# A graph layer on one core: the head of the kernel in an order set by hand, with a table of its own for the first quad of nodes

## The chip, the cores and the metric

The kernel runs on one core of a Trainium2 chip. The metric is device microseconds from the first to the last instruction of that core, as a median over runs; lower is better. The engines are named as in the profile: PE (matrix products, with PEld its weight loads), DVE (vector), ACT (scalar), POOL (GpSimd) and SP, which here only issues transfers. Each engine takes its instructions in the order in which the program gives them to it.

## The reference, cut to what matters

There are 12,500 nodes with 128 features and 412,500 edges. Edges are sorted by `dst`; `src` is in no order.

```
h    = relu(layernorm(x)) @ W_in2f
Wij  = (ssp(edge_attr @ W_f1 + b_f1) @ W_f2 + b_f2) * edge_weight[:, None]   # ssp(t) = softplus(t) - log 2
agg  = segment_sum(h[dst] * Wij, src, 12500)
out  = x + ssp(agg @ W_o1 + b_o1) @ W_o2 + b_o2
```

So each edge reads a row of `h` at its `dst`, multiplies it by a filter made from its 20 attributes, and adds the product to node `src`.

## The kernel before, in words

Nodes are worked on in 25 quads of 512 (the last one is shorter). `make_h(q)` is a generator that makes the rows of `h` for one quad in seven pieces: layer norm statistics on DVE (L310, L311) and the inverse root on ACT (L314, L315); the normalising on DVE (L326); transposes on PE (L331) and `relu` on ACT (L333); the product with `win` on PE (L337); then a split of the result into three bfloat16 parts, on ACT and DVE by turns (L339 to L345); then the stores on SP (L352, L359). The stores go to `h3`, and to tables `h3_q`, one for each quad: table q holds the rows of quad q with a margin of 256 rows before it and 384 after it. A quad therefore writes to up to three tables, and table 0 is complete only when quads 0 and 1 are both stored.

Edges are worked on in 806 chunks of 512, four chunks to a group. Since `dst` is sorted, the rows of `h` that a chunk needs lie in a window of 32 rows. `shift` holds where that window starts for each of the 808 chunks; `rel_d` holds, for each edge, its row within the window. Both come from `dst_c`: `relative()` computes `shift` from the first `dst` of each chunk (`first`, a load of 808 single elements, L155), and `rel` from seven loads of 128 chunks each (L160), which it writes to `rel_d` (L277). `ranges` checks later that all edges were in their windows.

`step(k)` issues the work of several chunks at different stages, in one fixed order. For chunk k + 12 the group's loads of attributes, `rel`, `src` and `edge_weight` (in `Group.__init__`, L542 to L556); for k + 6 the window load `near` (`rows`, L569 and L571), which reads a register from `shift`; for k + 7 and k + 6 the search for a free slot for each edge (`columns`, `blocks`, `rank`, `rank_end`: L578 to L606, L636, L655 and L687 on PE, L660); for k + 4 to k + 2 the first layer of the filter (`hidden`, `hidden_log`, `hidden_end`: L616, L619, L620, L625, L631); for k + 2 the selection matrix `at` (`window`, L706); for k + 1 the second layer of the filter `v` (L726, L730) and the picked rows `hg` (L714, L719); and for k the message: `o = v * hg` on DVE (L741), and four indirect stores on POOL (L745), each of which scatters 128 messages to their slots in `slots`. `o` has 4 buffers, each for two chunks, so that DVE waits at L739 for the scatters of eight chunks before. Later units of work (`Collect`) load the slots back and add them up with PE (L807), segment by segment, and `finish` makes the output. Its loads of `x` for the first three quads (`xo`, L387, and the addition of `bo2`, L401) need nothing from the loop, and stand at the head of the program.

The order of the head was left to the scheduler: constants, weights and their loads (on SP), the loads of `dst_c` (on ACT's queue), the bias parts (L246 to L253). Within `with tc.manual_schedule()` the order is the program's own:

```
h = [make_h(q, psum) for q in range(2)]
for m in h + h:
    next(m)
aside = side()
relative()
while h:                     # both quads to their end, by turns
    ...
for k in range(-LG, ...):    # LG = 12
    ...
    step(k, now)
    next(aside, None)
```

`side()` starts a further `make_h` every nine steps, from quad 2 on, beginning in step −12. Transfers issued from SP and ACT take eight semaphores in turn, so each transfer waits for the one eight before it in the program's order.

Of the kernel before, what the change touches and what calls it, by code (L numbers as in the profile page):

```python
# [31 lines left out]
EPS = 1e-5  # L32
NEAR = 2 * P
# [7 lines left out]
def gnn_kernel(  # L41
# [33 lines left out]
    NFLAG = 6 * len(SEGS) + 8  # L75
# [39 lines left out]
    ident = const.tile([P, P], F32, name="ident")  # L115
    make_identity(nc, ident)
    eps = const.tile([P, 1], F32, name="eps")
    nc.vector.memset(eps, EPS)
    half = const.tile([P, 1], F32, name="half")
    nc.vector.memset(half, 0.5)  # L120

    nc.scalar.preload_act_table_set("natural_log_exp_and_others")


    ln = ctx.enter_context(tc.tile_pool(name="ln", bufs=2))
    QN = QT * P
    NQ = ceil_div(N, QN)

# [12 lines left out]
    early = {q: load_x(q) for q in range(2)}  # L141

    state = ctx.enter_context(tc.tile_pool(name="state", bufs=1))
    early_room = state.tile([P, NTILE * P], F32, name="early_room", tag="agg")
    NC = NG * NCHUNK
    NPART = ceil_div(NG * NCHUNK, P)
    rel = early_room[:, NPART * CH:NPART * CH * 3 // 2 + CH].bitcast(BF16)
    rel = rel[:, :NPART * CH].rearrange("p (k e) -> p k e", e=CH)
    rows_at = NPART * CH * 3 // 2 + CH

    def early_row(k):
        return early_room[0:1, rows_at + k * NC:rows_at + (k + 1) * NC]

    first = early_row(0).bitcast(I32)
    nc.scalar.dma_start(first, dst_c[:, 0:1].rearrange("c o -> o c"))  # L155
    parts_c = []
    for c0 in range(0, NC, P):
        n = min(P, NC - c0)
        dc = early_room[:, len(parts_c) * CH:(len(parts_c) + 1) * CH].bitcast(I32)
        nc.scalar.dma_start(dc[:n, :], dst_c[c0:c0 + n, :])  # L160
        parts_c.append((c0, n, dc))


    quad_of = [min(c * CH * N // (n_edges * QN), NQ - 1) for c in range(NC)]

    def base_of(q):
        return max(0, q * QN - NEAR)

    def rows_of(q):
        return (q + 1) * QN + NEAR + P - base_of(q)  # L170

    base, last_w, strays, kept_in = (early_row(k) for k in range(1, 5))
    for q in range(NQ):
        cs = slice(quad_of.index(q), quad_of.index(q) + quad_of.count(q))
        nc.gpsimd.memset(base[:, cs], float(base_of(q)))
        nc.gpsimd.memset(last_w[:, cs], float(rows_of(q) - WR))

    def load(ap, shape, name):
        t = const.tile(shape, F32, name=name)
        nc.sync.dma_start(t, ap)  # L180
        return t

    win = load(w_in2f, [P, P], "win")

    before = const.tile([P, P], F32, name="before")
    nc.gpsimd.memset(before, 1.0)
    nc.gpsimd.affine_select(out=before, in_=before, compare_op=ALU.is_ge, fill=0.0, base=-1,
                            pattern=[[-1, P]], channel_multiplier=1)
    spare = const.tile([P, 1], F32, name="spare")
    nc.gpsimd.iota(spare, pattern=[[1, 1]], base=N, channel_multiplier=1,  # L190
                   allow_small_or_imprecise_dtypes=True)
    wf2 = load(w_f2, [P, P], "wf2")
    wo1 = load(w_o1, [P, P], "wo1")
    wo2 = load(w_o2, [P, P], "wo2")
    bf1 = load(b_f1[:, None], [P, 1], "bf1")
    bo1 = load(b_o1[:, None], [P, 1], "bo1")
    bf2 = load(b_f2[None, :].to_broadcast([P, P]), [P, P], "bf2")
    bo2 = load(b_o2[None, :].to_broadcast([P, P]), [P, P], "bo2")

    wf1 = const.tile([P, P], F32, name="wf1")  # L200
    for j in range(NCHUNK):
        nc.sync.dma_start(wf1[32 * j:32 * j + RBF, :], w_f1)

    def spread(t, n):
        return t[:, None, :].to_broadcast([t.shape[0], n, P])


    WP = 3 * WR
    prow_i = early_room[:WP, rows_at + 5 * NC:rows_at + 5 * NC + CH].bitcast(I32)
    nc.gpsimd.iota(prow_i, pattern=[[0, CH]], base=0, channel_multiplier=43)  # L210
    nc.vector.tensor_scalar(prow_i, prow_i, 7, None, op0=ALU.logical_shift_right)
    prow = const.tile([WP, CH], BF16, name="prow")
    nc.vector.tensor_copy(prow, prow_i)
    ones = const.tile([P, 1], F32, name="ones")
    nc.vector.memset(ones, 1.0)

    h3 = tc.dram_tile([NTILE * P, 3 * P], BF16, name="h3")
    h3_q = [tc.dram_tile([rows_of(q), 3 * P], BF16, name=f"h3_{q}") for q in range(NQ)]
    rel_d = tc.dram_tile([NC, CH], BF16, name="rel_d")
    flag = const.tile([1, 1], I32, name="flag")  # L220

    after = const.tile([P, P], F16, name="after")
    nc.gpsimd.memset(after, 1.0)
    nc.gpsimd.affine_select(out=after, in_=after, compare_op=ALU.is_ge, fill=0.0, base=-1,
                            pattern=[[1, P]], channel_multiplier=-1)
    nc.vector.scalar_tensor_tensor(after, ident, BIG, after, op0=ALU.mult, op1=ALU.add)

    rest_of = const.tile([P, P], F16, name="rest_of")
    nc.vector.tensor_scalar(rest_of, after, -1.0, 1.0, op0=ALU.mult, op1=ALU.add)
    ones_b = const.tile([P, P], BF16, name="ones_b")  # L230
    nc.vector.memset(ones_b, 1.0)

    turn = const.tile([P, NCHUNK, QT], F32, name="turn")
    for t in range(QT):
        nc.vector.memset(turn[:, :, t:t + 1], -1.0 if t % 2 else 1.0)
    places = const.tile([P, P], F32, name="places")
    nc.gpsimd.iota(places, pattern=[[1, P]], base=0, channel_multiplier=0,
                   allow_small_or_imprecise_dtypes=True)
    nbf1 = const.tile([P, 1], F32, name="nbf1")
    nc.vector.tensor_scalar(nbf1, bf1, -1.0, None, op0=ALU.mult)  # L240

    bf2_p = const.tile([3, P], BF16, name="bf2_p")
    left = const.tile([1, P], F32, name="bf2_left")
    with tc.tile_pool(name="bias_ps", bufs=1, space=PSUM) as bias_ps:
        b12 = bias_ps.tile([1, P], F32, name="b12")
        nc.tensor.matmul(b12, bf1, wf2, start=True, stop=True)  # L246
        nc.vector.tensor_add(left, b12, bf2[0:1, :])
    for k in range(3):
        part = const.tile([1, P], BF16, name=f"bf2_{k}")
        nc.vector.tensor_copy(part, left)  # L250
        if k < 2:
            nc.vector.tensor_sub(left, left, part)
        nc.sync.dma_start(bf2_p[k:k + 1, :], part)  # L253
    zero = const.tile([P, ZR * RW], F32, name="zero")
    nc.gpsimd.memset(zero, 0.0)
    bad = const.tile([1, NFLAG], F32, name="bad")
    nc.vector.memset(bad, 0.0)
    sums = tc.dram_tile([SUMT * P, P], F32, name="sums")
    segs = [Segment(k) for k in range(len(SEGS))]


    shift = const.tile([1, NC], I32, name="shift")

    def relative():
        nc.vector.tensor_sub(strays, first, base)
        nc.vector.tensor_scalar(kept_in, strays, 0.0, None, op0=ALU.max)
        nc.vector.tensor_tensor(kept_in, kept_in, last_w, op=ALU.min)
        nc.vector.tensor_copy(shift, kept_in)
        nc.vector.tensor_tensor(strays, strays, kept_in, op=ALU.not_equal)
        nc.vector.tensor_reduce(bad[:, NFLAG - 1:], strays,  # L270
                                axis=mybir.AxisListType.X, op=ALU.max)
        nc.vector.memset(rel[:, NPART - 1, :], 0.0)
        for k, (c0, n, dc) in enumerate(parts_c):
            d0 = ln.tile([P, 1], F32, name="d0")
            nc.vector.tensor_copy(d0[:n, :], dc[:n, 0:1])
            nc.vector.tensor_scalar(rel[:n, k, :], dc[:n, :], d0[:n, :], None, op0=ALU.subtract)
            nc.scalar.dma_start(rel_d[c0:c0 + n, :], rel[:n, k, :])  # L277

    def ranges(psum):
# [10 lines left out]
        nc.vector.tensor_reduce(worst, ends, axis=mybir.AxisListType.XY, op=ALU.max)  # L290
        nbad = psum.tile([P, QT, P], F32, name="nbad", tag="acc")[:1, 0, :1]
        nc.tensor.matmul(nbad, worst, ones, start=True, stop=True)
        nc.vector.tensor_copy(bad[:, NFLAG - 2:NFLAG - 1], nbad)


    none = const.tile([P, 3 * P], BF16, name="none")
    nc.vector.memset(none, 0.0)

    def make_h(q, psum):

        n = min(QT, NTILE - q * QT)
        xb = early.pop(q, None)
        if xb is None:
# [182 lines left out]
    with tc.tile_pool(name="edge", bufs=2) as edge, tc.tile_pool(  # L486
# [447 lines left out]
        def side():  # L934

            h = []
            for i in range(1000):
# [5 lines left out]
                if i == 40:  # L943
                    h.append(ranges(psum))
# [92 lines left out]
```

## Time and profile before

| what | value |
|---|---|
| median of 3 runs | 4383.54 us (4381.74 to 4402.45) |
| profiled execution, its own time | 4396.31 us |
| its span in the trace | 4394.5 us |
| mean granted clock of PE | 0.855 |
| busy: PE, DVE, ACT, POOL | 82%, 71%, 53%, 71% |
| transfers | 829.10 MB, mean 189 GB/s |
| first scatter starts, last scatter starts | 85.08 us, 4220.62 us |

In the rows of the timeline the columns are start and duration in microseconds, engine, line, operation and tiles; in brackets stands how long the engine had been idle and what ended that. In the rows of the windows they are the stretch, its length, the busy time of each engine with its number of instructions, the granted clock of PE, the busy share of the DMA engines and GB/s. An engine name with a q is the queue that issues for it.

### The profile page before, as it was taken

The page shows a single profiled execution, that of the slowest core. Times are in us where ns is not written, and L with a number is a line of the kernel's source. Part 1 is how long each engine was busy: PE and PEld are TensorE (multiplying, and loading weights), DVE is VectorE, ACT ScalarE, POOL GpSimd, SP SyncE. Part 2 cuts the span into 40 slices and gives each one's busy share as a digit, 9 for nine tenths or more (in the row PEclk, how much of TensorE's full clock was granted, in tenths as well). Part 3 has the DMA queues.
Part 4 walks back from the last instruction along what each step waited for, and adds up shares of the span by engine and source line. Part 5 has one row for each costly group of instructions (what it writes and reads, how often), then busy time and mean ns, then how long its engine had stood idle before and what let it go on. Part 6 is the DMA issues. An engine that isn't in the chain of part 4 may idle for free.

```text
span 4394.5 us, 72656 instructions
## 1 busy us (share of the span) xinstructions
PE 3607.4 (82%) x22558; PEld 2618.3 (60%) x22558; DVE 3140.1 (71%) x6637; ACT 2332.5 (53%) x4685; POOL 3114.6 (71%) x3288
## 2 busy tenths in 40 slices
PE   3767776777777888888788889999899998989877
PEld 2544444444444666666566567777677776767666
DVE  5766666566555776767667678787888878888766
ACT  3655555555555555555555555555555555545424
POOL 2777777677777777777777777777777777777620
PEclk9776666667666898899998899999999999999999
DMA  5766547888765666765876566666666766766666
GB/s 139 192 178 230 174 128 197 223 223 230 183 208 135 177 178 183 238 193 166 257 197 174 150 179 187 194 195 185 189 188 183 199 191 185 193 188 191 172 180 192
DMA packets 498071, 829.10 MB, mean 189 GB/s; under 512 B 170680, under 2 KB 288300, under 8 KB 497676
## 3 DMA queue, kind: packets, MB, share of 16 engines
q1 hardware_dynamic: 378950, 602.34, 51.2%
q0 software_dynamic: 103168, 213.15, 14.7%
q10 hardware_dynamic: 15558, 8.89, 0.7%
q8 instruction: 182, 2.98, 0.3%
q14 instruction: 213, 1.74, 0.1%
HBM read 425.03 MB, written 398.98 MB: 188 GB/s over the span
## 4 chain that ended last, share of the span: by engine, by line


## 5 line engine op out<-in xcount | busy, mean ns | idle before, releaser
L745 POOL DMA_INDIRECT slots<-o,slot x3224 | 3108.4, 964 | 1106.3 <-issue 803.6
L719 ACT ACTIVATE hg<-picked,rcut 128x128 f32<-128x128 f32 x3224 | 920.8, 369 | 1372.0 <-PE picked L714 1323.5
L807 PEld LDWEIGHTS acc<-to,m 128*128 128x128 f32 x8312 | 1078.7, 205 | 353.8 <-issue 187.7
L807 PE MATMUL acc<-to,m 128*128 128x128 f32 x8312 | 1154.6, 294 | 92.3 <-DVE agg L824 47.3
L730 PEld LDWEIGHTS v<-wf,r 128*128 128x128 f32 x6448 | 918.1, 220 | 303.7 <-issue 303.7
L730 PE MATMUL v<-wf,r 128*128 128x128 f32 x6448 | 1088.2, 320 | 0.0
L616 PE MATMUL z<-f,wf 20*128 20x512 f32 x1612 | 524.2, 726 | 217.5 <-DVE r L631 190.9
L794 DVE TENSOR_TENSOR to<-count_ps,m 128x768 f32<-128x768 f32 (+3 forms) x829 | 657.9, 812 | 51.8 <-PE acc L807 27.7
L619 ACT ACTIVATE a<-z,bf 128x1024 f32<-128x1024 f32 x403 | 449.1, 1114 | 426.7 <-PE z L616 426.7
L660 DVE TENSOR_REDUCE top<-free 128x4 f32<-128x392 f32 x806 | 447.2, 555 | 211.7 <-PE free L655 210.4
L631 DVE SCALAR_TENSOR_TENSOR r<-z,nbf,a 128x1024 f32<-128x1024 f32 x403 | 514.6, 1277 | 94.2 <-ACT a L625 92.5
L741 DVE TENSOR_TENSOR o<-v,hg 128x512 f32<-128x512 f32 x806 | 547.2, 679 | 2.8 <-ACT hg L719 2.1
L739 DVE COPY o<-place 128x8 f32<-128x8 f32 x403 | 80.4, 200 | 650.9 <-DMA slots<-o,slot 650.6
L714 PE MATMUL picked<-near,at 96*128 96x128 bf16 x3224 | 356.4, 240 | 218.0 <-DVE o L741 215.7
L625 ACT ACTIVATE a<-a,half 128x1024 f32<-128x1024 f32 x403 | 468.4, 1162 | 0.0
L636 DVE TENSOR_TENSOR inb<-count_ps,blk 128x392 f16<-128x392 f32 x806 | 445.7, 553 | 0.0
L726 PE MATMUL v<-bf_p,ones_b 3*128 3x512 bf16 x806 | 350.1, 434 | 104.1 <-DVE o L741 93.9
L620 ACT ACTIVATE a<-a 128x1024 f32<-128x1024 f32 x403 | 425.9, 1057 | 12.8
L714 PEld LDWEIGHTS <-at 96*128 96x128 bf16 x3224 | 275.7, 109 | 256.2 <-DVE o L741 224.6
L616 PEld LDWEIGHTS z<-f,wf 20*128 20x128 f32 x1612 | 142.4, 206 | 388.9 <-issue 186.3
L687 PE MATMUL free<-inb,rest_of 128*128 128x392 f16 x806 | 303.1, 376 | 55.0 <-DVE top L660 53.8
L706 DVE TENSOR_TENSOR at<-rel,prow 96x512 bf16<-96x512 bf16 x806 | 331.1, 411 | 0.0
(107 smaller groups left out, 1416.2 us busy)
## 6 DMA issues: line engine op xcount, KB each, us to landing
m<-slots SPq DMA_DIRECT2D x371, 387.0 KB
rel<-rel_d SPq DMA_DIRECT2D x202, 384.0 KB
m<-slots SPq DMA_DIRECT2D x172, 322.5 KB
m<-slots SPq DMA_DIRECT2D x212, 258.0 KB
slots<-o,slot POOLq DMA_INDIRECT x3224
slots<-zero SPq DMA_DIRECT2D x24, 2064.0 KB
f<-in_f_t SPq DMA_DIRECT2D x404, 80.0 KB
slots<-zero SPq DMA_DIRECT2D x22, 1032.0 KB
```

What stands on the lines that cost most here:

```text
L616: nc.tensor.matmul(z[:, k, :], wf1[rows, :], self.f[rows, :], start=True, stop=True)
L619: nc.scalar.activation(a, z, AF.Abs, bias=bf1)
L625: nc.scalar.activation(a, a, AF.Ln, bias=half, scale=0.5)
L631: nc.vector.scalar_tensor_tensor(r, z, nbf1, a, op0=ALU.max, op1=ALU.add)
L660: nc.vector.tensor_reduce(self.top[:, c * QT:(c + 1) * QT], free_v, axis=mybir.AxisListType.X, op=ALU.max)
L714: nc.tensor.matmul(ps[:, i, :], at[:, i * P:(i + 1) * P], near, start=True, stop=True)
L719: nc.scalar.activation(hg[:, i, :], ps[:, i, :], AF.Copy, scale=self.rcut[:, j:j + 1])
L730: nc.tensor.matmul(v[:, i, :], r[:, i * P:(i + 1) * P], wf2, start=False, stop=True, skip_group_check=True)
L741: nc.vector.tensor_mul(o[:, :, :P], v, hg)
L745: put = nc.gpsimd.indirect_dma_start(out=views[j % VIEWS], out_offset=bass.IndirectOffsetOnAxis(ap=self.slot[:, j:j + 1], axis=0), in_=o[: ...
L794: nc.vector.tensor_tensor(to[:, :n, :], count_ps[:, None, :].to_broadcast([P, n, P]), self.m[u][:, :n, P:].to_broadcast([P, n, P]), op=ALU ...
L807: nc.tensor.matmul(self.acc[b // QT][:, i, :], m[:, j, :P], to[:, j, :], start=t == 0, stop=t == self.seg.tiles(b) - 1)
```

## The change

The head is moved into functions that are called within the manual order. `constants()` loads quad 0 of `x`, the first part of `dst_c`, the first elements of 64 chunks (`FIRST`), `win`, `wf1` (all on SP), and `bf1`, `wf2`, `bf2` (on ACT), and sets the constants. Then come quad 0's first pieces, `relative(0)` and `shift(0)`, which serve 128 and 64 chunks. The loop over steps begins at that point: quad 0's other pieces, the loading and making of quad 1, and the bias parts (`biases`) are issued between the steps −12 to 0. `side()` begins in step 0. What is left goes into `rest()`, a generator which `side()` starts at its sixth call: the first elements of the other 744 chunks, `wo1`, `wo2`, `bo1`, `bo2`, `shift(1)` for 744 chunks, then the other six parts of `dst_c` one after another (load, `relative`, store), and at the end `ranges`. The loads and stores of `dst_c` and `rel_d` are now on SP's queue. In `Group.__init__` the load of `rel` comes after those of attributes, `src` and `edge_weight`.

There is a new first table, of the rows of quad 0 alone; chunks 0 to 8 use it. The other 25 tables are as they were. `make_h` stores to the new table first, and has one more piece after that.

The loads of `xo` stay at the head of ACT's queue, and the additions of `bo2` to them, which need `bo2`, now stand on DVE in step 8, between the operations of `shift(1)`.

```diff
+FIRST = 64
+    tables = [(0, QN)]
+    for q in range(NQ):
+        start = max(0, q * QN - NEAR)
+        tables.append((start, (q + 1) * QN + NEAR + P - start))
+    table_of = []
+    for c in range(NC):
+        n = c * CH * N // n_edges
+        table_of.append(0 if n < QN - NEAR - P else min(n // QN, NQ - 1) + 1)
...
-    early = {q: load_x(q) for q in range(2)}
...
+    def constants():
+        early[0] = load_x(0)
+        part_load(0)
+        first_load(0)
+        nc.sync.dma_start(win, w_in2f)
+        for j in range(NCHUNK):
+            nc.sync.dma_start(wf1[32 * j:32 * j + RBF, :], w_f1)
+        nc.scalar.preload_act_table_set("natural_log_exp_and_others")
+        nc.scalar.dma_start(bf1, b_f1[:, None])
+        nc.scalar.dma_start(wf2, w_f2)
+        nc.scalar.dma_start(bf2, b_f2[None, :].to_broadcast([P, P]))
+        make_identity(nc, ident)
+        bounds(0)
...
-        for j in range(max(0, q - 2), min(NQ, q + 2)):
+        for (b, rows), table in zip(tables, h3_t):
...
+                if b + rows == QN:
+                    yield
...
+                if g == 0:
+                    rel_store(0)
+                self.rel = edge.tile([WP, NCHUNK, CH], BF16, name="rel", bufs=4)
...
+        def rest():
+            first_load(1)
+            part_load(1)
+            late_loads()
+            for _ in range(3):
+                yield
+            shift(1)
+            for k in range(1, NPART):
+                relative(k)
+                if k + 1 < NPART:
+                    part_load(k + 1)
+                yield
+                yield
+                rel_store(k)
+                for _ in range(4):
+                    yield
+            yield from ranges(psum)
...
         with tc.manual_schedule():
+            constants()
+            nc.scalar.activation(count_ps, places, AF.Copy)
             h = [make_h(q, psum) for q in range(2)]
-            for m in h + h:
-                next(m)
+            next(h[0])
+            relative(0)
+            shift(0)
+            next(h[0])
+            next(h[0])
             aside = side()
-            relative()
-            while h:
-                for m in list(h):
-                    if next(m, 1):
-                        h.remove(m)
+            start = {-9: (1, 0), -7: (2, 0), -6: (0, 1), -5: (1, 1)}
+            start |= {k: (0, 1) for k in range(-4, 1)}
             for k in range(-LG, max(NCH, max(units) + 1)):
...
                 step(k, now)
-                next(aside, None)
+                if k == -LG:
+                    early[1] = load_x(1)
+                for m, n in zip(h, start.get(k, (0, 0))):
+                    for _ in range(n):
+                        next(m, None)
+                if k == -6:
+                    biases(psum)
+                if k >= 0:
+                    next(aside, None)
```

## The prediction, made before the changed kernel had run

> **What bounds the kernel now.** I read the page first. No engine is near 100% busy, so I looked for one whose gaps are its own. The costliest group is POOL's scatter:
>
> ```profile
> L745 POOL DMA_INDIRECT slots<-o,slot x3224 | 3108.4, 964 | 1106.3 <-issue 803.6
> ```
>
> One takes 0.96 us, and most of the idle time before them is "issue", time in which POOL waited for nothing. The table of waits and the table of windows (columns PE, PEld, DVE, ACT, POOL) came next:
>
> ```profile
> POOL slots L745 <- issue: 803.6, 2632, 0.9
> DVE o L739 <- DMA slots<-o,slot: 650.6, 198, 10.7
> POOL slots L745 <- DVE o L741: 109.4, 48, 78.2
> ...
> 800.00:900.00 100.00, 73.31 (x313) 45.48 (x314) 59.08 (x155) 50.00 (x103) 70.29 (x73) 0.59 0.89 231
> 1300.00:1400.00 100.00, 82.97 (x367) 50.64 (x366) 61.88 (x143) 58.34 (x117) 75.92 (x80) 0.62 0.51 138
> 3500.00:3600.00 100.00, 92.91 (x664) 73.13 (x662) 80.81 (x161) 54.79 (x111) 75.91 (x80) 0.95 0.69 193
> ```
>
> 79 to 80 scatters in 100 us, at PE clocks of 0.62 and 0.95 alike: one each 1.264 us (0.96 and a gap of 0.30). 3224 of them need 4075 us. DVE waits 650.6 us for scatters to free `o`; POOL waits 109.4 us for DVE, and 78.2 of that is one wait, the head's. So POOL, once started, sets the pace almost everywhere. Where it does not (800 to 900 us, DMA share 0.89; the last 100 us), the work hangs on the chunk number and moves with POOL's start. POOL's own rows give both ends:
>
> ```profile
> 85.08 1.11 POOL L745 DMA_INDIRECT slots<-o,slot  x1 [78.23 <-DVE o L741]
> 86.50 0.95 POOL L745 DMA_INDIRECT slots<-o,slot  x1 [0.30 <-issue]
> ...
> 4220.62 0.96 POOL L745 DMA_INDIRECT slots<-o,slot  x1 [0.31 <-issue]
> ```
>
> The span is 85.1 us of head, 4136.5 us from first to last scatter (61 above 4075), and 173 us of tail. A head shorter by t makes the kernel shorter by t, as long as POOL stays fed. Why the head takes 85 us stands in the timeline:
>
> ```profile
> 5.13 0.29 DVE L310 BATCH_NORM_STATS2 st<-xb 128x6 f32<-128x128 f32 x1 [3.67 <-DMA xb<-in_x]
> 13.43 0.30 ACT L314 ACTIVATE rs<-mv,eps 128x4 f32<-128x4 f32 x1 [11.33 <-DMA early_room<-in_dst_c]
> ...
> 33.11 0.60 ACT L333 ACTIVATE xT<-xps 128x512 f32<-128x512 f32 x1 [15.80 <-DMA rel_d<-early_room]
> ...
> 48.80 2.55 SPq L542 DMA_DIRECT2D f<-in_f_t  x4
> 51.40 0.33 SPq L547 DMA_DIRECT2D rel<-rel_d  x1
> 51.77 0.43 SPq L554 DMA_DIRECT2D src_i<-in_src_t  x1
> ...
> 58.18 0.29 DVE L310 BATCH_NORM_STATS2 st<-xb 128x6 f32<-128x128 f32 x1 [14.32 <-DMA xb<-in_x]
> ...
> 62.10 0.22 DVE L578 TENSOR_SCALAR part<-src_i 128x128 int32<-128x128 int32 x1
> ```
>
> ACT holds the statistics until 13.4 us, since it is busy issuing eight loads of `dst_c`; it holds the transposed `x` until 33.1 us, since it issues seven stores of `rel_d`, which wait for DVE. SP issues nothing for the edges until both quads' stores are out, at 48.8 us. DVE then starts on slots at 62.1, behind quad 2's statistics; 23.0 us later comes the first scatter.
>
> **The change, its cost part by part.** It takes seven of eight parts of ACT's issuing away, and lets the edge loads go before quad 0's stores. New work is small: one more store of 384 KB, to the new table. I follow the new order engine by engine, with durations of this trace.
>
> *To the edge columns.* Quad 0's `xb` lands at 5.1 (as now). Four pairs of statistics at a pitch of 0.40: 6.8. ACT has three `xo` issues ahead (0.42 each; the first waits for `xb`, the third for `win`); I put its Ln and Exp at about 9.1. `relative(0)` is 0.15 + 0.49; `shift(0)` is six operations, 5.07 us for 808 elements (L265 to L270); for 64 I take 0.2 each, from the smallest DVE rows. Normalising ends at 10.7 (four small ones, then 1.11); transposes 0.6 behind, xT 0.60, product 2.07, hb 0.60: 14.7. Meanwhile SP has issued `wf1`, `f` and `src`. `src` takes the turn of the second `xo`, which lands some 4.5 us after its issue (the third `xo` now: issued 16.96, awaited until 21.65). So `src` is issued at about 10.4 and lands near 14. Columns take 3.0 us (62.10 to 65.1): 17.0. One `inb` (0.56), then `left`, hb's second and third part (0.69, 0.62, 0.68): quad 0 goes to SP at 19.6. Its `near` loads have until 38 and are hidden, even at 4.3 us for the store and as much for the load (the first `xb` from issue to use).
>
> *To the first scatter.* DVE: `inb`, `top` (1.0), quad 1's statistics (1.6), bias parts (1.8; L240 and L247 to L250), `inb`, `top` (1.0), normalising (1.7): 26.7; two more `inb`/`top` (2.2), slots (0.6), `inb`: 30. PE's first hidden layer ends at 28.0. ACT: Abs, Exp, quad 1's xT, Ln (1.11, 1.06, 0.60, 1.16): 32.0. DVE: r 1.28, `at` 0.41: 33.7. PE: quad 1's product, `free`, second hidden layer (2.08): 35.9; v (0.6 + 2.08), picked 0.63: 39.2. ACT hg 1.14: 40.4, Ln 1.16: 41.6. In DVE's order the message stands behind `top`, quad 1's third part, `inb`, the second r (it needs that Ln; 1.28), `at` and a copy: 43.6. Message 0.68, POOL 0.30 later, as now: **first scatter at about 45 us**, 40 earlier.
>
> PE's clock is where a rule can be weighed. The rows:
>
> ```profile
> 77.74 2.08 PE L730 MATMUL v<-wf,r 128*128 128x128 f32 x8
> 90.29 1.16 PE L730 MATMUL v<-wf,r 128*128 128x128 f32 x8
> ```
>
> The same eight take 2.08 us early in the ramp and 1.16 after 12 us of denser work. By the mix of these rows, about half of the ramp's products (first hidden layer, quad 1's product) would run at the short time, and the first scatter would come at 42 to 43. The Trainium skill, "TensorE: Matmul & The Clock Gate", Part 1, has the array at half rate until it has been busy for about 3.4 us on end. The new ramp spreads PE's bursts of 1 to 3 us over 34 us, so by the rule all stay at the long time. I take the rule: 45 rather than 42.5.
>
> *What moves behind the start.* In step 8 DVE gets `shift(1)` (744/808 of 5.07 = 4.7), three `xo` additions (2.1; they were at 18.7 to 21.7) and one `relative` (0.64): 7.4 us in one place, and the message of chunk 9 waits behind them. Now the fifth pair's first message ends at 119.2 and its scatter is due at about 126, so DVE is 6.7 us ahead there; chunk 9 is due 5.1 later and its message 1.9 later. 7.4 + 1.9 fits into 6.7 + 5.1, with 2.5 to spare. With no such lead POOL would wait up to 7.4. I take 2.5. Five more `relative` and 14 reductions lie under DVE's waits for `o` (650.6 us); if that cover were gone they would cost their own time, about 3 + 7 us.
>
> SP's queue takes first elements (808 took 1.27 us to issue on ACT), `dst_c` parts, four weights, and six stores, each of which waits for DVE. Queued behind them are `near` loads, five steps (25 us) ahead of their use. I cost that at nothing; the lower bound is nothing too, since ACT's issues were all before the loop. How long 744 single elements occupy the queue is not in this trace: under 22.4 us for the 808 (issued at 0.85, DVE uses them at 23.29 without a wait), so within the 25. Transfers rise by 0.4 MB of 829; 2.3 MB of `dst_c` and `rel_d` traffic now falls into the loop, where the share is 0.6 to 0.7. The scatters, clears and tail are in the same order by chunk.
>
> **Sum:** 85.1 − 45 = 40 won, 2.5 given back: −38. Against the profiled execution's own time, 4396.3 − 38 = 4358. That execution lies 12.8 above the median of the runs, 4383.5; from the median the same is **4345**.
>
> **The rivals.** *(a) Same:* the first scatter comes late, or the start is paid back. The eight semaphores chain SP's loads to ACT's `xo`, and `columns`, `biases` and quad 1's pieces stand in DVE's only order; three waits of a landing (4.3 us) each on that chain, and 7.4 at step 8, leave 40 − 13 − 7 = 20, about 4363. For it: the head's waits now are of this kind, 11 to 16 us each. Against: the two that were long were ACT's issuing, which is gone.
>
> *(b) Slower:* the bound changes from POOL to PE in the stretch from 2600 to 4100 us, where PE is busy 88 to 94 us of 100 at a clock near 0.95. The clock decides: below about 0.95 × 0.91 = 0.87 PE needs more than POOL. At 0.80 it would need 91 × 0.95/0.80 = 108, so 8% of 1500 us: +120, less 38: about 4465. Against it: that order is unchanged, and the head's activity ends 2500 us before; other stretches at 0.62 kept POOL fed.
>
> *(c) The change doesn't do what it says:* a chunk waits for table 1 after all (chunk 9 on needs quad 1 stored). Its load is issued in step 3, after quad 1's stores, so at most one landing of 4.3 us: about 4350.
>
> **How the numbers follow.** 0.5%, or 21.9 us, is about what a measurement of this kernel can tell from no change. Main case, first scatter at 40 to 52, POOL fed: 0.72 (with c, 0.05 of it), 4336 to 4355. Rival (a): 0.21, of which a third still wins more than 22 (4355 to 4362) and two thirds stay within (4362 to 4383). Slower, (b) and the like: 0.07. Faster 0.79, same 0.14, slower 0.07. The range takes in the warm clock and a lead at step 8 below (4340) with a scatter of some us, and most of (a) above: 4330 to 4370.
>
> **What would show it.** Right: POOL's one long wait is near 38 us instead of 78.2; ACT's Ln for quad 0 starts before 10 us and its xT near 11; SP issues `src` near 10; 79 scatters in each window of 100 us from 100 us on; last scatter 38 us earlier; tail 173 us. Wrong: a first scatter after 60 us (then look at what DVE's `columns` or the first message waited for), gaps over 0.3 us in POOL between 80 and 110 us, behind `shift(1)`, or more than 61 us of gaps from first to last scatter.

## The result, and the profile after

The changed kernel takes 4343.44 us (median of 5 runs, 4343.14 to 4350.6) against 4384.4 for the kernel before (5 runs, 4381.74 to 4402.45) beside it: ratio 0.9911, 95% interval 0.9897 to 0.9924. That is 41 us less; 4345 was predicted. The profiled execution lies at the median this time (0.3 us below it): own time 4343.14, span 4341.3, mean granted clock of PE 0.855, as before.

First the page's row of the scatter, POOL's largest waits (total, times, longest) and three windows:

```profile
L772 POOL DMA_INDIRECT slots<-o,slot x3224 | 3115.4, 966 | 1052.9 <-issue 803.4
```

```profile
POOL slots L772 <- issue: 803.4, 2625, 1.6
DVE o L766 <- DMA slots<-o,slot: 646.6, 205, 10.8
...
POOL slots L772 <- DVE o L768: 62.8, 60, 33.3
```

```profile
700.00:800.00 100.00, 71.64 (x311) 44.87 (x311) 55.40 (x136) 49.46 (x102) 66.99 (x69) 0.60 0.87 232
1200.00:1300.00 100.00, 66.49 (x330) 39.69 (x327) 51.96 (x112) 52.19 (x106) 75.90 (x80) 0.69 0.62 205
3460.00:3560.00 100.00, 91.39 (x616) 71.83 (x615) 77.76 (x154) 51.36 (x101) 76.00 (x79) 0.90 0.62 183
```

One line changed: POOL's single long wait is 33.3 us instead of 78.2. The pace is what it was, 79 to 80 scatters in 100 us with PE at 0.69 and at 0.90; and the stretch with the DMA share of 0.87 (69 scatters) has not gone. It has moved with the chunk numbers: from 756 to 856 us there are 73 scatters, as there were from 800 to 900 us before. The two ends of POOL's row:

```profile
40.97 1.11 POOL L772 DMA_INDIRECT slots<-o,slot  x1 [33.30 <-DVE o L768]
...
4174.95 0.95 POOL L772 DMA_INDIRECT slots<-o,slot  x1 [0.30 <-issue]
```

| us | before | after | difference |
|---|---|---|---|
| first scatter starts | 85.08 | 40.97 | −44.1 |
| first to last scatter | 4135.5 | 4134.0 | −1.6 |
| behind the last scatter | 173.9 | 166.4 | −7.5 |

The three add up to −53.2, the difference of the two profiled spans; the medians differ by 41. The profiled run of before lay some 12 us above its median. The tail was 165.4 to 173.9 us in the profiles with a mean granted clock of 0.851 to 0.858, whichever kernel it was, so its 7.5 us are not a gain of the change.

The rows of the head, to be held against those of before:

```profile
4.37 0.29 DVE L333 BATCH_NORM_STATS2 st<-xb 128x6 f32<-128x128 f32 x1
6.66 0.28 ACT L337 ACTIVATE rs<-mv,eps 128x4 f32<-128x4 f32 x1
9.19 0.36 SPq L574 DMA_DIRECT2D src_i<-in_src_t  x1
11.05 0.60 ACT L356 ACTIVATE xT<-xps 128x512 f32<-128x512 f32 x1 [3.88 <-PE xps L354]
12.51 0.23 DVE L605 TENSOR_SCALAR part<-src_i 128x128 int32<-128x128 int32 x1 [2.02 <-DMA src_i<-in_src_t]
18.01 0.39 SPq L374 DMA_DIRECT2D h<-hb  x1
```

ACT's Ln starts at 6.66 instead of 13.43, xT at 11.05 instead of 33.11, and SP issues `src` at 9.19, nine us ahead of quad 0's store, instead of at 51.77. DVE starts on slots at 12.51 instead of 62.1.

The one thing in this profile that no step of the prediction had is a scatter of 5.23 us. These are the rows of POOL and of DVE in step 8:

```profile
79.00 5.23 POOL L772 DMA_INDIRECT slots<-o,slot  x1 [0.30 <-issue]
79.37 0.92 DVE L212 TENSOR_TENSOR early_room<-early_room 1x744 f32<-1x744 int32 x1
80.22 0.67 DVE L425 TENSOR_TENSOR xo<-xo,bo 128x512 f32<-128x512 f32 x1
80.82 0.53 DVE L213 TENSOR_SCALAR early_room<-early_room 1x744 f32<-1x744 f32 x1
81.27 0.67 DVE L425 TENSOR_TENSOR xo<-xo,bo 128x512 f32<-128x512 f32 x1
81.88 0.92 DVE L214 TENSOR_TENSOR early_room<-early_room 1x744 f32<-1x744 f32 x1
82.72 0.67 DVE L425 TENSOR_TENSOR xo<-xo,bo 128x512 f32<-128x512 f32 x1
83.32 0.53 DVE L215 CAST shift<-early_room 1x744 int32<-1x744 f32 x1
83.78 0.91 DVE L216 TENSOR_TENSOR early_room<-early_room 1x744 f32<-1x744 f32 x1
84.54 1.00 POOL L772 DMA_INDIRECT slots<-o,slot  x1 [0.30 <-issue]
```

POOL does not wait here: the bracket says 0.30, its usual gap, and that is why the table of waits shows nothing. The scatter itself lasts 5.23 us instead of 0.96, while DVE runs one operation straight after another (each row starts before the one above has fully ended), most of them with two inputs in SBUF. That is 4.3 us in the row that sets the pace. The longest scatter of before was 1.44 us.

### The profile page after: what moved, and what is told of

It is laid out like the page before. It is cut to its first block, busy times and chain, and to the rows that moved or that the text cites. A ratio compares the mean times of both kernels' runs of the same rounds, so it can differ in the third digit from the quotient of the medians.

```text
span 4341.3 us, 72669 instructions
## 1 busy us (share of the span) xinstructions
PE 3615.0 (83%) x22558; PEld 2623.8 (60%) x22558; DVE 3143.0 (72%) x6643; ACT 2328.5 (54%) x4685; POOL 3122.2 (72%) x3292
## 4 chain that ended last, share of the span: by engine, by line
## 5 line engine op out<-in xcount | busy, mean ns | idle before, releaser
L766 DVE COPY o<-place 128x8 f32<-128x8 f32 x403 | 77.7, 193 | 646.7 <-DMA slots<-o,slot 646.6
L741 PE MATMUL picked<-near,at 96*128 96x128 bf16 x3224 | 357.2, 240 | 177.0 <-DVE o L768 173.7
```

Of the source, the lines that this page charges most:

```text
L741: nc.tensor.matmul(ps[:, i, :], at[:, i * P:(i + 1) * P], near, start=True, stop=True)
```

## The experiments

There are eleven runs in three series, each series beside the kernel before; the changed kernel and the one with a shorter head are each among them twice. The theory: POOL's row of scatters sets the end, so a first scatter earlier by t is worth t; the head was long because ACT and SP issued transfers ahead of what the first scatter needs. In the first series before had 4382.24 us (18 runs). In the second series both kernels were slower (PE's mean granted clock was 0.735 to 0.744 in the profiles, before took 5816.5 us, and POOL waited 1579 us for DVE in the changed kernel), so times of that series are compared only within it.

**ACT's queue alone.** Before, with one edit in three lines:

```diff
-    nc.scalar.dma_start(first, dst_c[:, 0:1].rearrange("c o -> o c"))
+    nc.sync.dma_start(first, dst_c[:, 0:1].rearrange("c o -> o c"))
...
-        nc.scalar.dma_start(dc[:n, :], dst_c[c0:c0 + n, :])
+        nc.sync.dma_start(dc[:n, :], dst_c[c0:c0 + n, :])
...
-            nc.scalar.dma_start(rel_d[c0:c0 + n, :], rel[:n, k, :])
+            nc.sync.dma_start(rel_d[c0:c0 + n, :], rel[:n, k, :])
```

> The kernel before, with one edit: the eight loads of dst_c and the seven stores of rel_d are issued by SP instead of ACT. Theory (the long head was above all ACT's issuing): ACT takes quad 0's Ln near 8 us and xT near 12 instead of 13.4 and 33.1, the quads' stores go out near 25 instead of 43, and the first scatter comes at 65 to 70 us instead of 85; time about 4366. Rival (the order is what counts: edge loads behind both quads' stores, all of shift and rel ahead of them): first scatter at 80 to 85, time as before, 4384.

Measured: 4365.5 us, ratio 0.997 (0.9949 to 0.9991). From the timeline:

```profile
19.38 0.60 ACT L333 ACTIVATE xT<-xps 128x512 f32<-128x512 f32 x1 [11.32 <-PE xps L331]
39.02 0.43 SPq L554 DMA_DIRECT2D src_i<-in_src_t  x1
72.35 1.11 POOL L745 DMA_INDIRECT slots<-o,slot  x1 [65.51 <-DVE o L741]
```

ACT's Ln comes at 5.78 instead of 13.43 with ACT's issues gone, and xT 13.7 us earlier; xT waits for PE (behind DVE's normalising) now, no longer for a transfer. The first scatter is 12.7 us earlier, 2 to 7 less than expected: SP issues the same loads instead, and `src` still stands behind the stores of the quads. So moving ACT's issues is worth 12.7 of the 44 us by itself. The larger part is left to the order, which the next edits take apart.

**Interleaving undone.** After, with both quads and the bias parts made to their end before step −12, as before had it, and quad 1 of `x` loaded at the head for that:

```diff
         early[0] = load_x(0)
+        early[1] = load_x(1)
...
-            next(h[0])
-            next(h[0])
+            next(h[1])
+            while h:
+                for m in list(h):
+                    if next(m, 1):
+                        h.remove(m)
+            biases(psum)
             aside = side()
...
-                if k == -LG:
-                    early[1] = load_x(1)
-                for m, n in zip(h, start.get(k, (0, 0))):
-                    for _ in range(n):
-                        next(m, None)
-                if k == -6:
-                    biases(psum)
```

> The changed kernel with the interleaving undone: quads 0 and 1 and the bias parts are done to their end before step -12, the rest as it is. Theory (edge loads must not stand behind the quads' stores on SP): src is issued at 23 to 26 us instead of 9.2 and the first scatter comes at 50 us, time about 4352. Rival (quad 1's 5 us of DVE work leave the ramp, so the ramp is shorter by as much): first scatter 45 to 46, time 4348.

Measured: 4362.8 us, ratio 0.9956 (0.9933 to 0.9979).

```profile
33.99 0.36 SPq L575 DMA_DIRECT2D src_i<-in_src_t  x1
37.33 0.23 DVE L606 TENSOR_SCALAR part<-src_i 128x128 int32<-128x128 int32 x1 [12.23 <-DMA src_i<-in_src_t]
...
60.60 1.11 POOL L773 DMA_INDIRECT slots<-o,slot  x1 [52.93 <-DVE o L769]
```

The first scatter is 19.6 us later than in the changed kernel, and 10.6 later than expected. SP issues `src` 24.8 us later, since the stores of quad 0 and quad 1 and of the bias parts stand ahead of it and wait for DVE; DVE idles 12.23 us for it. From DVE's first work on `src` to the first scatter it is 23.3 us, 5.2 less than in the changed kernel (28.5), where DVE makes quad 1 in that time; that much of the rival holds.

**The table alone.** The same, and chunks 0 to 8 read the old table:

```diff
-        table_of.append(0 if n < QN - NEAR - P else min(n // QN, NQ - 1) + 1)
+        table_of.append(min(n // QN, NQ - 1) + 1)
```

> As the kernel with both quads first, and without the use of the new table: chunks 0 to 8 read the old table of quad 0, which needs both quads stored. Theory (the table saves nothing by itself, it only permits quad 1 to be made later): the same first scatter within 1 us and the same time. Rival (the first windows wait for the last store of that table): 3 to 4 us later.

Measured: 4358.1 us, ratio 0.9941 (0.992 to 0.9962), first scatter at 59.99. The table by itself saves nothing that shows (the first scatter is 0.6 us the other way, and the two intervals overlap). What it does is to allow quad 1 to be made later, which the interleaving uses.

**Deferral undone.** After, with all first elements, both shifts and all seven parts of `dst_c` ahead of the loop again:

```diff
         first_load(0)
+        first_load(1)
...
+        for k in range(1, NPART):
+            part_load(k)
...
                 if g == 0:
-                    rel_store(0)
+                    for part in range(NPART):
+                        rel_store(part)
...
             shift(0)
+            shift(1)
+            for k in range(1, NPART):
+                relative(k)
```

> The changed kernel with the deferral undone: first elements of all chunks, all seven parts of dst_c, their relative and shift for all 808 chunks are done where the first 64 chunks' are; only the weights stay late. Theory (deferral is worth what it takes off DVE and SP): DVE has 4.7 + 6 x 0.64 = 8.5 us more ahead of quad 0's normalising, SP 13 more issues of some 0.4; first scatter at 50 to 55 us instead of 41, the long scatter of step 8 gone (4.3 won back), time about 4350. Rival (it lies under waits for src and the clocked chain): first scatter 42 to 44, time 4340.

Measured: 4348.2 us, ratio 0.9917 (0.9885 to 0.9949). The timeline, with the scatter nearest to the additions of `bo2`:

```profile
48.79 1.11 POOL L776 DMA_INDIRECT slots<-o,slot  x1 [41.12 <-DVE o L772]
...
89.42 0.68 DVE L428 TENSOR_TENSOR xo<-xo,bo 128x512 f32<-128x512 f32 x1
89.71 1.92 POOL L776 DMA_INDIRECT slots<-o,slot  x1 [0.30 <-DVE top L710]
...
90.11 0.68 DVE L428 TENSOR_TENSOR xo<-xo,bo 128x512 f32<-128x512 f32 x1
```

The deferral is worth 7.8 us of first scatter. (ACT's 12.7, the interleaving's 19.6 and these 7.8 come from edits at different kernels, so they need not add up to 44.1.) And here, where `shift(1)` is out of step 8, no scatter takes 5 us: the one under the three additions takes 1.92.

**What holds the scatter.** The second shift spread over six steps, one operation each (`shift` gets a `yield` behind each of its operations):

```diff
-            shift(1)
+            yield from shift(1)
```

> The changed kernel with shift(1)'s six operations (4.7 us on DVE) in six steps, one each, instead of all in step 8; the three additions of bo2 stay together. Theory (a run of DVE operations with both inputs in SBUF holds up the scatter that POOL is executing): the scatter of 5.2 us in step 8 is gone, none is over 2 us, and from first to last scatter it takes some 3 to 4 us less; time 4340. Rival (something else of step 8 does it, such as the load of 744 single elements or the start of a new phase): one scatter of about 5 us stays; time 4343.

Measured: 5766.7 us, ratio 0.994 (0.991 to 0.9969) to the before of the second series. Runs of one kernel differ by 36 to 72 us in that series, so its times tell nothing about 4 us, and only the profiles are used.

```profile
95.08 1.63 POOL L778 DMA_INDIRECT slots<-o,slot  x1 [1.99 <-DVE o L774]
95.79 0.92 DVE L212 TENSOR_TENSOR early_room<-early_room 1x744 f32<-1x744 int32 x1
...
104.17 0.91 DVE L216 TENSOR_TENSOR early_room<-early_room 1x744 f32<-1x744 f32 x1
104.26 1.67 POOL L778 DMA_INDIRECT slots<-o,slot  x1 [0.30 <-issue]
```

The long scatter is gone; one alone under a two-input operation of 744 elements takes 1.63 or 1.67, and the longest (1.89, at 99.53) is the one under the `xo` additions. The load of the 744 elements is where it was, so that is not what holds the scatter.

The second shift done twice in a row:

```diff
             shift(1)
+            shift(1)
```

> The changed kernel with shift(1) computed twice in step 8. Theory (the scatter waits for DVE's run of two-input operations to end): the long scatter grows from 5.2 to about 10 us, by the 4.7 us of the second one; time 4348. Rival (a load, or POOL waiting for chunk 9's message): the scatter itself stays at 5.2 us; POOL would show an idle wait for DVE of up to 5 us behind it instead.

Measured: 5789.1 us, ratio 0.9961 (0.9933 to 0.9989).

```profile
92.86 5.58 POOL L772 DMA_INDIRECT slots<-o,slot  x1 [1.12 <-DVE o L768]
...
100.04 1.60 POOL L772 DMA_INDIRECT slots<-o,slot  x1 [0.30 <-issue]
101.94 1.22 POOL L772 DMA_INDIRECT slots<-o,slot  x1 [0.31 <-issue]
...
106.95 0.96 POOL L772 DMA_INDIRECT slots<-o,slot  x1 [3.78 <-DVE o L768]
```

This is not what I expected: the long scatter doesn't grow. It is 5.58 us, the same as in the unchanged order of that series (below). The second shift stretches two scatters, to 1.60 and 1.22, and then POOL waits 3.78 us for the message, which is DVE's own delay. The difference between the two shifts: the first has the `xo` additions between its operations and no gap; in the second there are gaps of 0.03 to 0.04 us between most of them. I changed the theory to: a scatter is held while DVE runs *without a gap*, and gets in at the first one.

To test that, the load of `bo2` was put later, so that the additions leave the shift (third series):

```diff
         nc.sync.dma_start(bo1, b_o1[:, None])
+
+    def last_bias():
         nc.sync.dma_start(bo2, b_o2[None, :].to_broadcast([P, P]))
...
                 rel_store(k)
+                if k == 1:
+                    last_bias()
```

> The changed kernel with one load moved: that of the output bias (one 128x128 transfer) is issued behind part 1 of the relative indices instead of with the other late loads, so the three additions of the bias to the output rows no longer stand among the six operations of the second shift on VectorE; the six keep their order and stand alone. Theory (a GpSimd scatter is held while VectorE runs operations with two SBUF inputs without a gap between them; the six alone depend on each other, and each leaves a small gap): the first scatter stays at 41.0, no scatter between 75 and 95 us takes more than 2.0 us, and the first scatters get 3 us of the 4.3 back; the time is about 3 us below the changed kernel's, 4340. Rival one (what counts is the total of such work in a step, with or without gaps, so the six alone, 4.5 us long, hold the scatter for most of their length): one scatter of 3.5 to 4.5 us there, 4343. Rival two (it is the transfers of the late loads on the DMA queues that hold the scatter, not VectorE): one scatter of about 5 us stays where it is.

> The changed kernel as it is, beside the other two of this call, for a comparison on one chip. First scatter 40.7 to 41.0, one scatter of 5.2 to 5.6 us near 79 to 93 us, ratio to the kernel before 0.991 where POOL sets the pace.

```profile
75.31 1.30 POOL L774 DMA_INDIRECT slots<-o,slot  x1 [0.30 <-issue]
75.69 0.91 DVE L212 TENSOR_TENSOR early_room<-early_room 1x744 f32<-1x744 int32 x1
76.64 0.54 DVE L213 TENSOR_SCALAR early_room<-early_room 1x744 f32<-1x744 f32 x1
76.91 1.10 POOL L774 DMA_INDIRECT slots<-o,slot  x1 [0.30 <-DVE early_room L212]
77.28 0.92 DVE L214 TENSOR_TENSOR early_room<-early_room 1x744 f32<-1x744 f32 x1
78.24 0.54 DVE L215 CAST shift<-early_room 1x744 int32<-1x744 f32 x1
78.32 1.29 POOL L774 DMA_INDIRECT slots<-o,slot  x1 [0.30 <-issue]
78.70 0.92 DVE L216 TENSOR_TENSOR early_room<-early_room 1x744 f32<-1x744 f32 x1
...
95.07 3.24 POOL L774 DMA_INDIRECT slots<-o,slot  x1 [0.30 <-DMA slots<-o,slot]
...
96.81 0.67 DVE L427 TENSOR_TENSOR xo<-xo,bo 128x512 f32<-128x512 f32 x1
```

The same six operations in the same order, without the additions among them, now let the scatters through at 1.10 to 1.30 us each; the unchanged order beside it held one for 5.17 us (at 76.43). So it is not the amount of the shift's work, and rival one falls; rival two falls for the late loads that stayed where they were. (The load of `bo2` moved along, but it is done before the additions start, and the hold lasts through them.) The second half is a miss: the additions, now from 95.09 on between a quad's statistics, hold another scatter for 3.24 us. In all the scatters from 75 to 99 us lose 3.1 us instead of 4.5, so 1.4 came back and not 3. The first scatters came at 40.74 here and 40.87 beside it. In time nothing can be told: 4350.0 us (6 runs, ratio 0.992, 0.9902 to 0.9937) against 4351.4 for the changed kernel (5 runs, 0.9918, 0.9903 to 0.9932) and 4387.7 for before (11 runs).

The edit took away two things at once, the missing gaps and the additions, and the profiles speak for the additions. The scatter at 78.32 got through in 1.29 us although L216 follows L215 without a gap (78.24 + 0.54 = 78.78, and L216 starts at 78.70). And the scatter of 5.23 us in the changed kernel ended at 84.23, while DVE's row had its first gap only at 84.69 (behind L216). What the end of a held scatter does follow is the last addition of `bo2` in the row (three of them, two with the shorter head):

| profile | held scatter, us | ends behind the end of the last addition, us |
|---|---|---|
| changed kernel; in the third series | 5.23; 5.17 | 0.84; 0.85 |
| in the second series; with the shift twice | 5.58; 5.58 | 0.84; 0.85 |
| interleaving undone; the same, without the table | 5.05; 4.91 | 0.85; 0.84 |
| additions apart from the shift | 3.24 | 0.83 |
| deferral undone; second shift spread | 1.92; 1.89 | 0.84; 0.86 |
| shorter head (below), twice | 2.38; 1.94 | 0.84; 0.84 |

So the hold lasts until the last of the additions, whatever follows. With the shift's operations between them the three additions took from 80.22 to 83.39, 3.2 us, against 2.05 us where they stand by themselves (deferral undone). In the one case seen where one stands apart it holds nothing: in the second profile of the shorter head the third addition stands 1.8 us behind the other two, and the scatter that starts in it takes 0.96. Why a scatter does not get in between two additions while other operations run there (up to 0.8 us in the changed kernel), and whether a gap there would let it in, was not tried.

**A shorter head still.** `src` and `rcut` loaded right behind the first `x`, quad 0's normalising ahead of `relative(0)`, quad 1 made in steps −3 to 3, `side()` from step 4, the second shift spread:

```diff
         early[0] = load_x(0)
...
+        nc.sync.dma_start(src_0[:, :w], src_t[:, :w])
+        nc.sync.dma_start(rcut_0[:, :w], rcut_t[:, :w])
...
-            next(h[0])
+            for _ in range(3):
+                next(h[0])
             relative(0)
...
-            start = {-9: (1, 0), -7: (2, 0), -6: (0, 1), -5: (1, 1)}
-            start |= {k: (0, 1) for k in range(-4, 1)}
+            start = {-9: (1, 0), -7: (2, 0), -5: (1, 0)}
+            start |= {k: (0, 1) for k in range(-3, 4)}
```

In the second series, beside the changed kernel once more:

> The changed kernel with shift(1) in six steps, src and edge_weight of the first group loaded right after quad 0's x, quad 0's normalising ahead of relative(0) and shift(0) on DVE, quad 1 made three steps later (steps -3 to 3), and side() begun in step 4. Theory (DVE's one order is what the first scatter waits for: 2.0 us for src, 1.9 for relative and shift, 4.7 for quad 1): first scatter at 34 to 36 us instead of 41, no long scatter; time 4333. Rival (PE's and ACT's chain of the first chunks is as long by itself, or quad 1 in the first steps starves POOL): first scatter 39 to 41 or gaps of some us in POOL behind it; time 4340 to 4345.

> The changed kernel itself, on the same chip as the three others, as their reference: first scatter at 41 us, the 5.2 us scatter in step 8 again if it comes from the order of the instructions; time 4343.

Measured: 5761.9 us, ratio 0.9915 (0.9881 to 0.9949), first scatter at 37.23, 1 to 3 us later than expected; the changed kernel 5778.9 us, ratio 0.9942 (0.9916 to 0.9968), first scatter at 40.73, with its long scatter of 5.58 us. The changed kernel is 37.6 us faster than before there too, although POOL's own row does not set the pace through that run. In the third series:

> The shorter head once more (source indices and cut-off loaded right behind the first x rows, the first quad's normalising ahead of the relative indices and the first shift, the second quad between steps -3 and 3, the remainder from step 4, the second shift in six steps), on one chip with the changed kernel. Theory (POOL paces everything behind its first scatter, so a head gain carries over one for one): first scatter at 37.2, 3.7 earlier than the changed kernel's, 2 to 3 more from the scatter that is no longer held: 4337, ratio to the changed kernel 0.9985 to 0.999. Rival (the end is set by something other than POOL's row of scatters by now, or the second quad's work, moved among the steps, delays as much as it wins): 4343.

```profile
37.34 1.12 POOL L786 DMA_INDIRECT slots<-o,slot  x1 [29.92 <-DVE o L782]
...
80.47 1.94 POOL L786 DMA_INDIRECT slots<-o,slot  x1 [0.31 <-issue]
```

Measured: 4344.5 us (6 runs, ratio 0.9906, 0.9891 to 0.9921) against 4351.4 for the changed kernel: 6.9 us or 0.16% less by the medians, where some 6 us were expected; the profiles show 3.5 us of head (37.34 against 40.87) and 3.2 us of the long scatter (1.94 against 5.17). The two intervals overlap, and the means differ by 5.8 with a standard error of 2.4 us: likely, not settled.

The head gain and the time, side by side (the first scatter against the one profile of before, the median against the before of its series: first 4382.24, third 4387.66):

| kernel | first scatter earlier by | median lower by |
|---|---|---|
| ACT's queue alone | 12.7 | 16.7 |
| interleaving undone | 24.5 | 19.4 |
| the same, without the table | 25.1 | 24.1 |
| deferral undone | 36.3 | 34.0 |
| changed kernel, third series | 44.2 | 36.2 |
| additions apart, third series | 44.3 | 37.7 |
| shorter head, third series | 47.7 | 43.2 |

One us of head is worth about one us of time throughout, with a scatter of 1 to 8 us.

## Why the prediction was right

- **The bound, and that a head gain carries over.** Right. POOL's row began 44.1 us earlier and ended 45.7 us earlier, and the table above has the same for the other heads.
- **To the edge columns: 17.0 predicted, 15.4 measured.** `xb` landed at 4.37 instead of 5.1, ACT's Ln came at 6.66 rather than 9.1, `src` was issued at 9.19 (10.4) and was there at 12.51 (14). DVE did wait for it, 2.02 us. The 0.2 us taken for each operation of `shift(0)` were 0.18 to 0.21. `relative(0)` was put too short: its second operation took 1.49 us instead of 0.49, in a stretch in which POOL filled `early_room`; that lay under DVE's wait for `src`. (ACT issues no part of `dst_c` any more, where the prediction leaves it one of eight; no figure rests on that.)
- **To the first scatter: 45 predicted, 40.97 measured.** 1.6 of the 4.0 are those above. Behind the columns I had 0.4 too much to quad 1's normalising (24.75), 0.3 to ACT's Ln (29.75), and 1.7 to `picked` (35.30): I let the second layer wait for the whole of the next hidden product (to 35.9), but PE had run that by 33.5.
- **PE's clock.** The choice was right and its reason wasn't, so this was luck. All the products of the ramp ran at the long time, to the last before the first scatter:

```profile
33.43 2.08 PE L757 MATMUL v<-wf,r 128*128 128x128 f32 x8
...
41.75 1.16 PE L757 MATMUL v<-wf,r 128*128 128x128 f32 x8
```

  But the ramp is not made of bursts of 1 to 3 us. From the window of this trace, and one of before:

```profile
28.76:40.10 11.34, 11.34 (x44) 7.34 (x44) 7.51 (x15) 6.84 (x12) 0.00 (x0) 1.00 0.36 101
```

```profile
78.00:90.00 12.00, 12.00 (x49) 7.69 (x49) 6.63 (x18) 8.49 (x18) 3.99 (x4) 0.50 0.70 163
```

  PE is busy for all of the 11.34 us, and products took the long time to the end of them; in before they did so from 75.73 to 89.96. So 3.4 us of busy PE on end, the figure that the prediction takes from its rule, were not enough in either trace, and the measurement decides (with the reserve that the profile models where a product ends). The granted clock reads 0.50 in the stretch of before and 1.00 in that of after, so in this trace it does not show the long time. What ended it at 40 us stays open. The 42.5 us of the other choice would have been closer to 40.97, but by an error that offsets another one.
- **2.5 us given back at step 8.** The step that failed in its mechanism, within its bounds of 0 and 7.4. I looked for POOL waiting for a late message; the prediction's own sum leaves 2.5 us to spare there, which is no loss, and the 2.5 us given back were a choice between the bounds. DVE's lead was indeed enough: POOL has no idle time over 0.31 us between 41 and 330 us. The loss is 4.3 us inside one scatter, so that its size comes near is luck. The Trainium skill, "SBUF — State Buffer", "SBUF: two separate sides", describes a hold of this kind: VectorE and GpSimd share one pair of SBUF ports under an exclusive lock, the one that starts first keeps it for its whole instruction, and a VectorE operation with two SBUF inputs takes part only against a GpSimd operation that reads SBUF. The prediction did not weigh that. Whether the scatter, whose offsets lie in SBUF, is such an operation no run here shows, so the lock is a candidate for the cause and not a finding. By that page a scatter is held for the length of one instruction; here it was held across a row of them, until the last addition.
- **Covers at nothing.** Held. DVE's waits for `o` are 646.6 us (650.6 before), so the five other `relative` and the reductions lie under them; and of the 177.0 us of PE's idle time before `picked`, 176.1 end on DVE or ACT, none worth naming on a `near` load.
- **The rivals.** (a) fell: of the engines' waits that end on a transfer before the first scatter there are two, DVE's 2.02 us for `src`, and 4.34 us of ACT for `win`, which ends at 6.44, 0.4 us behind the statistics that ACT's Ln needs. (c) fell with POOL's unbroken row. (b) was not set off: the window at 3460 us has a clock of 0.90 and 79 scatters. In the second series, at 0.74, the kernel before took one third more time than elsewhere and POOL waited for messages, where I had put 120 us at 0.80; but PE was busy only 73% of that span, so it is not the saturation that (b) supposed, and its cause wasn't tried. It met both kernels alike.
- **The sum.** −38 stands for 44.1 less 4.3, and 41 by the medians. That the 4.3 us don't show in the stretch from first to last scatter (1.6 shorter, not longer) is the variation of single executions: the changed kernel had 4134.0 and 4140.7 there, and the other profiles of the first and third series 4116 to 4137.

## What to carry to other kernels

Find the engine whose gaps are its own, and look at what its first instruction waits for: here the head was not short of compute, it was short of the right order in two issue queues, and one us of head was one us of time. A store that waits for its data holds every load behind it in its queue (with the interleaving undone `src` went out 24.8 us later), so the loads that the first useful step needs go ahead of the first such store. When work is moved beside a busy GpSimd, do not put a row of VectorE operations with two inputs in SBUF in one place: with the shift spread over six steps no scatter took over 2.4 us. And look at the durations of GpSimd's instructions, since a held one shows no idle time.

## What the runs showed of the hardware that was not expected

- An indirect store on POOL of 0.96 us takes 4.9 to 5.6 us where VectorE runs three additions of 128x512 elements, both inputs in SBUF, with other operations close between them, and 1.9 to 3.2 us under two or three of them in a row without the shift's operations. In all eleven profiles with such a row it ends 0.83 to 0.86 us behind the end of the last addition. It isn't every busy stretch of VectorE: most of its work here has an input in PSUM, and scatters under that stay at 0.96; the shift's operations of 1x744 elements alone stretch them to 1.1 to 1.7 us.
- PE's products took the long time (2.08 us for eight) through 11 to 14 us of PE without an idle gap.
- The kernel before took 4382 us in one series and 5816 us in another, where the mean granted clock of PE in the profiles was 0.74 instead of 0.855. The record lists the same chip number for both, so what differed is not shown. The change saved 36 to 41 us elsewhere and 37.6 us there.
